# Two attention layers on one core: the first layer's projection as seven products of quarters

## The chip, the core and the metric

The kernel runs on one NeuronCore of a Trainium2 chip. The core has a matrix engine (TensorE, PE in the profile; its weight loads are listed apart as PEld), a vector engine (VectorE, DVE), an activation engine (ScalarE, ACT), a general engine (GpSimd, POOL) and a sequencer that mostly issues transfers (SyncE, SP). Each engine works through its own instruction queue in order; the queues meet only through semaphores. Matmuls write to PSUM, a small memory of banks of 512 four-byte columns on 128 partitions; the other data lie in SBUF, which is 128 partitions wide, or in DRAM. The metric is the time of one execution on the device in microseconds (us).

## The reference

An input of 8 images with 512 channels of 32 x 32 points (1024 tokens) passes through two attention layers. In what follows b is the image ("batch"), C = 512 channels, T = 1024 tokens.

```python
# layer 0: 8 heads of 64 channels
h   = group_norm(x)                            # 32 groups of 16 channels
qkv = einsum('oc,bct->bot', qkv_w, h) + qkv_b
q, k, v = fake_quant(each)                     # 8 bits, range over the whole tensor
w = softmax(q' k * scale);  a = w v            # per head, 1024 x 1024
x = x + einsum('oc,bct->bot', proj_w, a) + proj_b      # the projection

# layer 1: one head of 512 channels
h = group_norm(x)
q, k, v = h wq + bq, h wk + bk, h wv + bv
attn = softmax(q k / sqrt(512));  out = attn v
x = x + out wp + bp
```

The change concerns the line of the projection: a 512 x 512 matrix times 512 channels x 1024 tokens per image, added to the image and a bias per output channel, and the group norm's statistics that are taken from the result.

## The kernel before, in words

A first stage computes q, k and v of all images and keeps them in DRAM. A second stage interleaves the two layers: the generator `attention` runs layer 0's heads for one image ahead, and `others` runs the projection, the second norm and layer 1 for the image before it. Each time `others` yields, one step of `attention` is issued: four score tiles (`scores`, the tiles `st`), their exponentials on ScalarE (`pt`), the split of each into a half-precision cast and a remainder (`two`; the cast on ScalarE, GpSimd or VectorE, the remainder always on VectorE), the products with v (`over_keys`, tiles `av`) and the row sums (`totals`, tiles `sm`). `yield 2` makes the step begin with the products (`late`), `yield -1` makes it begin with two score tiles (`dense`).

The matmul order is the program's own. On VectorE and ScalarE a planner decides: `dve.do` places work at once, and `dve.later` puts a chore with a cost and a due time on a list, from which `fill` takes what fits before the next placed work; `settle` forces all chores of a name. The plan becomes a fixed order of each engine's queue. `awaits` tells the planner when a tile is free; it is no instruction.

Large matrix products outside layer 0 use `seven`: operands in quarters, seven products in place of eight, with sums and differences of quarters made ahead and the results added up in two PSUM tiles x and y that take turns; `keep`, `add` and `whole` empty a tile after each product. Layer 1's products are done so: `g` (a_block), `v2ps` (v_block2), `s` (s_block) and `o` (o_run). In these, `keep` is a copy on ScalarE.

The projection, `project` (line 1296), is not: for each half of the tokens (512 columns) and each of four blocks of 128 output channels it adds four matmuls of 512 columns in one PSUM tile `pj`, and VectorE adds tile, bias and image in one instruction into the image's tile `h` (`evict`, line 1313). A store of the result to DRAM (`x1_d`) and the norm's statistics (`stats`) follow. The weights `wp` come from the input by a 1 MB transfer on ScalarE's queue (`load_wp`, line 1266), for image 0 in pieces on SP's queue (`load_first`). For images 1 to 7 the projection sits inside layer 1 of the image before: in `o_run`, after the fourth of seven products of its second half, `between[0]` (function `first`) runs one attention step, the projection's first half, a step, the second half, and then a `late` step; then comes the fifth product of `o`, and after it the first part of the norm (`norm1`, `norm_steps`). That part is a small matmul `gps` of the channel means with a matrix that averages over groups, then four small VectorE steps, then a second small matmul. PSUM tiles for the projection come from the pool of the score tiles (two tiles of 2 x 512 columns, `score_bank`), for image 0 from the pool `ps_o`.

In the profile all VectorE and ScalarE work carries line 91 and all matmuls line 209, so the names of the tiles tell the steps apart.

## Time and profile before

| quantity | value |
|---|---|
| median of 3 runs | 2557.06 us (2555.32 to 2558.21) |
| profiled execution | 2557.22 us, its span 2555.4 us |
| granted TensorE clock | 0.999 |
| projection matmuls `pj` | 224.0 us busy, in 512 records (256 matmuls) |
| evictions `h<-pj,vec,h` on VectorE | 64, mean 750 ns |
| statistics | 690 ns each, the aggregate 210 ns |
| 1 MB weight transfers `wp` | 7, on ScalarE's queue |
| stores `x_d<-h` | 64 of 256 KB, on SP's queue |
| transfers in all | 250.70 MB, 98 GB/s on average |

The projections can be found in time by their tiles: image 0 from 692.9 us, image 1 from 930.9 and then one every 240 us or so, image 7 from 2363.6. The profile's lines give start and length, engine, instruction, shapes, and in brackets the idle time of the engine before and what ended it. A matmul of four-byte numbers appears as two records, and records of one group overlap, so the spacing of the starts is the better measure of cost. From image 3 on, some matmul records are missing from the trace.

### The profile page before, as it was taken

The numbers are of one execution on the slowest core, as the hardware profiler recorded it, in microseconds if no ns is written. First come the engines' busy times: TensorE is split into PE (matmuls) and PEld (weight loads), VectorE is DVE, ScalarE is ACT, GpSimd is POOL, SyncE is SP. The second block draws the span as 40 slices with busy tenths as digits, with TensorE's granted clock in tenths as the row PEclk, the third lists the DMA queues.
The fourth block names the chain that finished last, engine by engine and source line by source line (L and its number), as shares of the span: only waits on it lengthen the run. The fifth ranks groups of instructions, "written<-read, shape, count | busy, mean of one in ns | idle before, by whom it ended". The sixth has DMA issues, their size and how long they took to land.

```text
span 2555.4 us, 38727 instructions
## 1 busy us (share of the span) xinstructions
PE 2516.6 (98%) x15670; PEld 1746.1 (68%) x15670; DVE 1895.6 (74%) x2746; ACT 1348.2 (53%) x1687; POOL 187.9 (7%) x167
## 2 busy tenths in 40 slices
PE   8999999999999999999999999999999999999998
PEld 4788888873357756775777577657756775777687
DVE  7888776668887778777877787777778777775544
ACT  3332223219856655665667466656665675664122
POOL 0000000001100001000100100010101000100000
PEclk9999999999999999999999999999999999999999
DMA  4533333236622232223223222322232123212211
GB/s 167 178 142 124 132 124 121 110 130 164 164 88 63 79 113 87 59 70 127 92 59 104 84 87 74 109 96 63 80 109 91 55 72 124 87 51 84 87 38 39
DMA packets 160718, 250.70 MB, mean 98 GB/s; under 512 B 27153, under 2 KB 93713, under 8 KB 159121
## 3 DMA queue, kind: packets, MB, share of 16 engines
q1 hardware_dynamic: 125792, 182.81, 21.9%
q10 hardware_dynamic: 30560, 57.71, 6.6%
q0 software_dynamic: 4176, 7.60, 1.7%
q8 instruction: 125, 2.05, 0.3%
q14 instruction: 65, 0.52, 0.1%
HBM read 153.64 MB, written 86.28 MB: 94 GB/s over the span
## 4 chain that ended last, share of the span: by engine, by line
PE 85%; DVE 4%; issue 3%; ACT 2%; DMA 1%; POOL 0%; SPq 0%; ACTq 0%; DVEq 0%; POOLq 0%
PE s L209 15%; PE o L209 13%; PE qkps L209 12%; PE pj L209 8%; PE av L209 8%; PE v2ps L209 7%; PE g L209 6%; PE vps L209 6%; PE st L209 4%; PE sm L209 3%; ACT pt L91 1%; DVE two L91 1%; DVE h L91 1%; PE fold L209 0%; DVE acc L91 0%
## 5 line engine op out<-in xcount | busy, mean ns | idle before, releaser
L91 ACT ACTIVATE pt<-st,esc 128x1024 f32<-128x1024 f32 x467 | 497.1, 1115 | 332.7 <-PE st L209 316.8
L91 DVE TENSOR_TENSOR two<-pt,two 128x1024 f16<-128x1024 f32 x467 | 561.9, 1217 | 131.5 <-POOL two L1092 100.8
L91 ACT CAST two<-pt 128x1024 f16<-128x1024 f32 x346 | 350.8, 1056 | 6.9 <-ACT p L91 5.1
L1092 POOL CAST two<-pt 128x1024 f16<-128x1024 f32 x112 | 147.5, 1317 | 1406.8 <-PE sm L209 745.1
L209 PE MATMUL av<-two,v 128*32 128x512 f16 x3968 | 245.7, 381 | 2.5 <-DVE two L91 2.4
L209 PE MATMUL s<-g,h 128*128 128x256 f32 x1024 | 233.4, 380 | 0.0
L209 PE MATMUL pj<-ao,wp 128*128 128x512 f32 x512 | 224.0, 595 | 0.6 <-DVE h L91 0.6
L209 PEld LDWEIGHTS s<-g,h 128*128 128x128 f32 x1024 | 192.9, 190 | 31.0 <-issue 4.3
L91 ACT ACTIVATE u_ring<-qkps,qkbt 128x512 f32<-128x512 f32 x89 | 61.1, 687 | 243.6 <-PE qkps L209 228.9
L209 PEld LDWEIGHTS <-v 128*32 128x32 f16 x3968 | 92.0, 96 | 139.8 <-issue 66.7
L209 PEld LDWEIGHTS pj<-ao,wp 128*128 128x128 f32 x512 | 96.0, 190 | 122.5 <-issue 112.2
L209 PE MATMUL s<-g,sums 128*128 128x256 f32 x768 | 178.4, 381 | 0.2 <-DVE p L91 0.2
L209 PE MATMUL o<-p,v 128*128 128x256 f32 x768 | 175.2, 382 | 1.0 <-DVE p L91 1.0
L209 PE MATMUL st<-q,k 64*128 64x512 bf16 x1024 | 163.4, 382 | 12.2 <-ACT pt L91 7.8
L209 PEld LDWEIGHTS o<-p,v 128*128 128x128 f32 x768 | 144.3, 190 | 27.1 <-issue 5.7
L209 PEld LDWEIGHTS s<-g,sums 128*128 128x128 f32 x768 | 144.6, 190 | 24.3 <-issue 4.6
L209 PE MATMUL sm<-two,ones 128*32 128x512 f16 x1984 | 136.0, 379 | 0.0
L209 PEld LDWEIGHTS <-k 64*128 64x128 bf16 x1024 | 34.8, 94 | 144.1 <-issue 142.5
L209 PE MATMUL qkps<-half,w_high 128*128 128x512 f32 x480 | 132.5, 398 | 0.0
L209 PE MATMUL qkps<-half,w_mix 128*128 128x512 f32 x480 | 130.6, 394 | 1.0 <-DVE half L91 1.0
L209 PE MATMUL qkps<-half,w_low 128*128 128x512 f32 x480 | 130.5, 394 | 0.0
L209 PE MATMUL v2ps<-wm,h 128*128 128x256 f32 x512 | 119.9, 383 | 1.9 <-ACT g L91 1.3
(228 smaller groups left out, 3903.9 us busy)
## 6 DMA issues: line engine op xcount, KB each, us to landing
rs<-rs_d SPq DMA_DIRECT2D x76, 256.0 KB
x<-in_x_dram SPq DMA_DIRECT2D x32, 512.0 KB
q_d<-wa SPq DMA_DIRECT2D x32, 512.0 KB
k_d<-wa SPq DMA_DIRECT2D x32, 512.0 KB
v_d<-v_ring SPq DMA_DIRECT2D x32, 512.0 KB
raw<-q_d SPq DMA_DIRECT2D x32, 512.0 KB
raw<-k_d SPq DMA_DIRECT2D x32, 512.0 KB
x_d<-h SPq DMA_DIRECT2D x64, 256.0 KB
```

The lines of the kernel that those rows point to most:

```text
L91: ins = self.latest = op(*args, **kw).ins
L209: ins = nc.tensor.matmul(ps, lhsT=lhsT, rhs=rhs, **kw).ins
L1092: copy(two[:, 0], pt)
```

## The change

For images 1 to 7 the projection is computed by `seven`, half by half: the weights' quarters a11, a12, a22 and the sums s1 to s4 on the left, the attention result's quarters and differences on the right. The left operands are made once, during image 0's projection, from its weights (`combine_wp`: four additions on VectorE) and kept in a DRAM tile `wp_d` by four stores; each later image loads six of the seven in one transfer of 1.5 MB and the seventh, s4, apart, into a free part of layer 1's v tile. The right operands are made on VectorE: t1 in place soon after the second pair of heads is divided (`first_sums`), t2 in the v tile at the start of the projection, t3 and t4 in place after the first and second product of each half. Each of the seven products is added by VectorE straight into a quarter of the image's tile, without a copy on ScalarE; the option `alone` of `seven` gives these calls their own turn-taking. Statistics of two channel blocks become due after the sixth product and of the other two after the seventh.

Image 0 keeps the eight products.

The bias is no longer added in the eviction. `norm_steps` takes it as `shift`: it is added to the channel means before the group matmul, and taken off the group mean that is later subtracted from the data. The residual image stored in DRAM then lacks the bias, so it is added to the output bias `ob`.

```diff
--- before.py
+++ after.py
@@ -226,7 +226,8 @@
     def norm_steps(
-        src, dst, wcol, bank, nm, ccs=range(CC), fine=False, put=None, mv=None, apply=None
+        src, dst, wcol, bank, nm, ccs=range(CC), fine=False, put=None, mv=None, apply=None,
+        shift=None,
     ):
@@ -242,6 +243,8 @@
                 if fine and i + 1 < n:
                     yield
         yield
+        if shift is not None:
+            dve.tensor_add(mv[:, :, 0], mv[:, :, 0], shift)
         ps = bank(f"gps_{nm}")[:, 0:n]
         mm(ps, lhsT=gavg, rhs=mv[:, :, 0], start=True, stop=True)
@@ -250,7 +253,10 @@
         def offsets():
             dve.tensor_sub(d, mv[:, :, 0], ps)
-            dve.tensor_copy(mean, ps)
+            if shift is None:
+                dve.tensor_copy(mean, ps)
+            else:
+                dve.tensor_sub(mean, ps, shift)
             dve.tensor_mul(d, d, d)
             dve.tensor_add(d, d, mv[:, :, 1])
@@ -1184,6 +1190,8 @@
                 def divide():
                     dve.scalar_tensor_tensor(aot, aot, scl[:, 2:3], rs, ALU.mult, ALU.mult)
+                    if b and j == 1:
+                        first_sums(b)
                 def spread():
                     r = rcs[:, n * 16 : (n + 1) * 16]
@@ -1264,8 +1272,8 @@
                 dma(xts[b][:, :, bass.ts(hf, 512)], x_v[b, :, :, bass.ts(hf, 512)])
         def load_wp(b, dma):
-            wps[b] = l2p.tile([P, CC, C], F32, tag="sums", name=f"wp0_{b}")
-            dma(wps[b], w_sq[WP0])
+            wps[b] = w = l2p.tile([P, 6, CC // 2, C // 2], F32, tag="sums", name=f"wp0_{b}")
+            dma(w, wp_d[:, 0:6])
         def load_first(u):
@@ -1293,11 +1301,108 @@
             for t, src in zip(wm_tiles(b), wm_d):
                 act.dma_start(t, src)
-        def project(b, bank=bank):
+        wp_d = dram.tile([P, 7, CC // 2, C // 2], F32, tag="wp", name="wp_d")
+        def combine_wp():
+            wc = l2p.tile([P, 3, NT // 2, 256], F32, tag="vsum", name="wp_combined").rearrange(
+                "p a (s k) n -> p (a s) k n", k=2
+            )
+            a11, a12, a21, a22 = (
+                wps[0][:, k * CC // 2 : (k + 1) * CC // 2, m * 256 : (m + 1) * 256]
+                for m in range(2) for k in range(2)
+            )
+            s2, s3, s1, s4 = (wc[:, i] for i in range(4))
+            for args in (
+                (s1, a21, a22, ALU.add), (s2, s1, a11, ALU.subtract),
+                (s3, a11, a21, ALU.subtract), (s4, a12, s2, ALU.subtract),
+            ):
+                dve.later("wc", elements(512), lambda args=args: tt(*args), within=20.0)
+            def keep():
+                nc.sync.dma_start(wp_d[:, 3:7], wc[:, 0:4])
+            dve.later("wc", 0.0, keep, within=20.0)
+            nc.sync.dma_start(wp_d[:, 0], a11)
+            nc.sync.dma_start(wp_d[:, 1], a12)
+            nc.sync.dma_start(wp_d[:, 2], a22)
+        def first_sums(b):
+            for cc in range(CC // 2):
+                h = ao[b, cc]
+                dve.later("at", elements(512), lambda h=h: tt(
+                    h[:, :, 256:512], h[:, :, 256:512], h[:, :, 0:256], ALU.subtract
+                ), within=30.0)
+        def project_seven(b, room):
+            settle("at")
             settle("ao")
+            st, mvs[b] = stat_tiles(CC, f"b{b}")
+            w = wps.pop(b)
+            a11, a12, a22, s2, s3, s1 = (w[:, i] for i in range(6))
+            t2 = room[:, 0 : NT // 2, 0:256].rearrange("p (k h) n -> p k h n", h=NH)
+            s4 = room[:, NT // 2 : NT // 2 + 2, 0:256]
+            nc.sync.dma_start(s4, wp_d[:, 6])
+            left, right = slice(0, 256), slice(256, 512)
+            def second(k):
+                tt(t2[:, k], ao[b, 2 + k][:, :, right], ao[b, k][:, :, right], ALU.subtract)
+            for k in range(2):
+                dve.do(elements(512), lambda k=k: second(k))
+            for hf in range(NH):
+                h11, t1, h21, h22 = (
+                    [ao[b, c + k][:, hf, n] for k in range(2)] for c in (0, 2) for n in (left, right)
+                )
+                th = [t2[:, k, hf] for k in range(2)]
+                q11, q12, q21, q22 = quarters(b, hf)
+                def into(q, row, col, full, hf=hf):
+                    def add(ps):
+                        there = dve.do(elements(512), lambda: tt(q, ps, q, ALU.add))
+                        if full is not None:
+                            nc.sync.dma_start(x1_d[b][row][hf][:, :, col * 256 : (col + 1) * 256], q)
+                        return there
+                    return add
+                def stats(oc, hf=hf):
+                    dve.bn_stats(st[:, oc, hf, :], xts[b][:, oc, bass.ts(hf, 512)])
+                    if hf == NH - 1:
+                        aggregate(mvs[b], st, oc)
+                keeps = [into(q, *at_, None) for q, at_ in ((q11, (0, 0)), (q21, (1, 0)), (q22, (1, 1)))]
+                adds = [into(q, *at_, 1) for q, at_ in ((q11, (0, 0)), (q21, (1, 0)), (q22, (1, 1)))]
+                for step in seven(
+                    f"pj_{b}_{hf}",
+                    ((a11, h11), (a12, h21), (s2, th), (s3, h11), (s1, t1), (s4, h22), (a22, h21)),
+                    lambda n, ps: keeps[n](ps), into(q12, 0, 1, 1), lambda n, ps: adds[n](ps),
+                    score_bank, True,
+                ):
+                    if step in (1, 2):
+                        for k in range(2):
+                            h = (h11, h21)[step - 1][k]
+                            args = (h, th[k], h) if step == 1 else (h, h, th[k])
+                            dve.do(elements(256), lambda args=args: tt(*args, ALU.subtract))
+                    for oc in {6: (2, 3), 7: (0, 1)}.get(step, ()):
+                        dve.later("pj", 0.62 + 0.2 * hf, lambda oc=oc, stats=stats: stats(oc), within=4.0)
+                    chore()
+                if hf + 1 < NH:
+                    yield -1
+            for k in [k for k in ao if k[0] == b]:
+                del ao[k]
+        def project(b, room=None):
+            if b:
+                yield from project_seven(b, room)
+                return
+            settle("ao")
+            combine_wp()
             st, mvs[b] = stat_tiles(CC, f"b{b}")
             wp0 = wps.pop(b)
             for hf in range(NH):
@@ -1311,9 +1416,7 @@
                     xx = xts[b][:, oc, bass.ts(hf, 512)]
                     def evict():
-                        dve.scalar_tensor_tensor(
-                            xx, ps, vec[:, V_PB0 + oc : V_PB0 + oc + 1], xx, ALU.add, ALU.add
-                        )
+                        dve.tensor_tensor(xx, ps, xx, ALU.add)
                         nc.sync.dma_start(x1_d[b][oc // 2][hf][:, oc % 2, :], xx)
                     def stats(oc=oc, hf=hf, xx=xx):
@@ -1359,9 +1462,11 @@
                     put(hf, elements(512), work)
             for n, _ in enumerate(norm_steps(
-                at, at, V_GN1W, bank, f"b{b}", put=put, mv=mvs[b]
+                at, at, V_GN1W, bank, f"b{b}", put=put, mv=mvs[b], shift=vec[:, V_PB0 : V_PB0 + CC]
             )):
                 if n == 2:
+                    if b == 0:
+                        settle("wc")
                     sums[b] = l2p.tile(
                         [P, 3, NH, CC // 2, 256], F32, tag="sums", name=f"sums2_{b}"
                     )
@@ -1390,14 +1495,15 @@
             dve.later("o", 0.25, spread, pe.t + 4.0, 5.0)
             return rs
-        def seven(nm, pairs, keep, whole, add, bank=bank):
+        def seven(nm, pairs, keep, whole, add, bank=bank, alone=False):
             nonlocal turn
-            turn ^= 1
+            turn ^= not alone
+            free, side = ([0.0, 0.0], 0) if alone else (busy, turn)
             x, y = (bank(f"{nm}_{i}").rearrange("p (t n) -> p t n", t=2) for i in range(2))
             def product(n, ps, start):
@@ -1406,7 +1512,8 @@
                 for t in range(2):
                     for i in range(k):
                         mm(
-                            ps[:, t, :], lhsT=left[:, i, bass.ts(t, P)], rhs=right[:, i, :],
+                            ps[:, t, :], lhsT=left[:, i, bass.ts(t, P)],
+                            rhs=right[i] if type(right) is list else right[:, i, :],
                             start=start and t == 0 and i == 0, stop=(i == k - 1),
                             skip_group_check=True,
                         )
@@ -1417,12 +1524,14 @@
                 (5, x, False, whole, None),
             )
             for i, (n, ps, start, out, m) in enumerate(work):
-                awaits(free[(i + turn) % 2])
+                if not alone:
+                    side = turn
+                awaits(free[(i + side) % 2])
                 product(n, ps, start)
-                free[(i + turn) % 2] = out(ps) if m is None else out(m, ps)
+                free[(i + side) % 2] = out(ps) if m is None else out(m, ps)
                 yield i + 1
-        free = [0.0, 0.0]
+        busy = [0.0, 0.0]
         turn = 0
         def slots(gq):
@@ -1773,8 +1882,9 @@
                     def first():
                         nonlocal ahead
                         yield -1
-                        yield from project(b + 1, score_bank)
+                        yield from project(b + 1, vt)
                         yield 2
+                        settle("pj")
                         ahead = norm1(b + 1, score_bank)
                         next(ahead)
@@ -1856,6 +1966,7 @@
                     load_first(24)
                 else:
                     dve.tensor_add(dst, tot, vec[:, V_BP : V_BP + CC])
+                    dve.tensor_add(dst, dst, vec[:, V_PB0 : V_PB0 + CC])
             (m11, m12), (m21, m22), (v1, v2), (v3, v4) = ([t[:, i] for i in range(2)] for t in wm)
             for args in (
                 (v1, m11, m12, ALU.subtract), (v2, m22, v1, ALU.subtract),
```

## The prediction

> **What bounds the kernel now.** First the page's totals, then who TensorE waited for, then the order of time around one projection. The totals:

> ```profile
> PE 2516.6 (98%) x15670; PEld 1746.1 (68%) x15670; DVE 1895.6 (74%) x2746; ACT 1348.2 (53%) x1687; POOL 187.9 (7%) x167
> ```

> TensorE is busy for 98% of the span at a granted clock of 0.999: time is won only by fewer or shorter matmuls, and lost wherever a matmul waits. The list of TensorE's waits is short:

> ```profile
> PE st L209 <- ACT pt L91: 7.8, 15, 0.8
> PE gps_a L209 <- DVE gmv_a L91: 6.9, 1, 6.9
> PE st L209 <- DVE h L91: 3.1, 6, 0.5
> PE av L209 <- DVE two L91: 2.4, 4, 1.6
> ```

> No entry is a transfer. The third is the projection's: six times, 0.52 us each. Here is batch 1 on TensorE, then on VectorE (start, length, instruction, idle before). Two records of a 4-byte matmul are one matmul, so x32 is 16:

> ```profile
> 930.91 14.00 PE L209 MATMUL pj<-ao,wp 128*128 128x512 f32 x32
> 944.84 0.39 PE L209 MATMUL st<-q,k 64*128 64x512 bf16 x2
> 945.75 0.39 PE L209 MATMUL st<-q,k 64*128 64x512 bf16 x2 [0.52 <-DVE h L91]
> ...
> 949.43 14.00 PE L209 MATMUL pj<-ao,wp 128*128 128x512 f32 x32
> 963.36 1.05 PE L209 MATMUL av<-two,v 128*32 128x512 f16 x16
> ...
> 967.27 3.72 PE L209 MATMUL o<-g,vsum 128*128 128x256 f32 x16
> 970.83 0.28 PE L209 MATMUL gps_b<-gmv_b,gavg 128*128 128x4 f32 x2
> 970.97 3.70 PE L209 MATMUL o<-g,v 128*128 128x256 f32 x16
> ```

> ```profile
> 957.39 0.69 DVE L91 BATCH_NORM_STATS2 gst_b<-h 128x6 f32<-128x512 f32 x1
> 958.12 0.21 DVE L91 BATCH_NORM_AGGREGATE gmv_b<-gst_b 128x2 f32<-128x12 f32 x1
> 958.24 1.17 DVE L91 TENSOR_TENSOR two<-pt,two 128x1024 f16<-128x1024 f32 x1
> ...
> 963.47 0.75 DVE L91 SCALAR_TENSOR_TENSOR h<-pj,vec,h 128x512 f32<-128x512 f32 x1 [0.70 <-PE pj L209]
> ...
> 971.03 0.69 DVE L91 TENSOR_TENSOR kept_u<-o,kept_u 128x512 f32<-128x512 f32 x1 [2.78 <-PE o L209]
> 971.64 0.15 DVE L91 TENSOR_TENSOR gd_b<-gmv_b,gps_b 128x4 f32<-128x4 f32 x1
> ```

> To be seen: from the last projection matmul to the matmul of the means (gps) TensorE passes 970.83 - 963.36 = 7.47 us and never waits; VectorE stands idle for 2.78 us ahead of 971.03, so it has room, but its order is fixed. The prices of the two matmul shapes come from undisturbed runs:

> ```profile
> 1041.75 3.62 PE L209 MATMUL s<-g,h 128*128 128x256 f32 x16
> 1045.20 1.89 PE L209 MATMUL s<-g,sums 128*128 128x256 f32 x8
> ...
> 2363.60 27.63 PE L209 MATMUL pj<-ao,wp 128*128 128x512 f32 x64
> 2391.06 3.62 PE L209 MATMUL o<-g,vsum 128*128 128x256 f32 x16
> ```

> A 512-column matmul costs (2391.06 - 2363.60)/32 = 0.858 us, a 256-column one (1045.20 - 1041.75)/8 = 0.431.

> **The change, part by part.**

> *Seven products.* Half a batch was 16 matmuls of 512 columns, 13.73 us; it becomes 28 of 256, 12.08. Gain 1.65 per half, in batches 1 to 7, so 14 times: **-23.1 us**. All of it is on the path.
> [...]

> *Evictions.* VectorE now empties a tile seven times per half, not four, and each product reuses the tile of the one but last. A product lasts 4 x 0.431 = 1.73 us. An eviction begins 0.11 after its product (944.84 to 944.95) and takes 0.69 (TENSOR_TENSOR from the accumulator, 128x512), so it is late only if VectorE reaches it over 0.93 us late. Between evictions stand two subtractions on 256 columns or one 0.75 us quantisation step. No row has a tensor-tensor on 256 columns; it lies between 0.44 (scalar-tensor-tensor on 256) and 0.69 (tensor-tensor on 512), nearest the former by size: two take 0.88, and 0.11 + 0.61 + 0.88 = 1.6 fits in 1.73. Even two at 0.69 would overrun one slot by 0.3, within the 0.93. **Zero**, covered by the next product.
> [...]

> *End of the first half.* The second score tile still waits for the last eviction; that is now 0.69, not 0.75: -0.06 in six batches, **-0.4**. Behind it VectorE has three cast remainders ("two", 1.13 from start to start), three statistics (0.61) and one scaling (0.61) before the next half's first eviction: 0.72 + 3.39 + 1.83 + 0.61 = 6.55 after the product, due at 4.53 + 1.73 + 0.11 = 6.37. Late by 0.2, inside the 0.93.

> *End of the second half, batches 1 to 6.* This is the price. The planner moves four cast remainders and three statistics behind the last eviction, and the new add stands behind one more remainder and behind the eviction of the next attention product; gps waits for the add, and everything on TensorE waits behind gps. From the last projection matmul: eviction 0.11 + 0.61 = 0.72; four remainders 4 x 1.13, to 5.24; three statistics with aggregate at 0.85 (957.39 to 958.24), to 7.79; a remainder, to 8.92; eviction of o, there since about 8, to 9.53; add 0.15 (row gd_b), 9.68; gps 0.06 later, 9.74. Against 7.47 that is 2.27 us, and a wait of about 0.5 of "av" for the second remainder hides inside. **+13.6** in six batches. Bounds: had all statistics drained earlier, only the o eviction and the add remain, 0.11 + 0.61 + 0.15 + 0.06 = 0.93 a batch, 5.6 in all; were the remainders as slow as 1.35 (5.46 for four at 751.88), 1.1 more each, 20 in all. I take the middle, since the row's mean of 467 is 1.217 long, 1.13 spaced.

> *Batch 7* has no attention left beside it: the chain is 3.27, the o product ends at 3.46 (2391.06 to 2394.52), then 0.93: **+0.9**.

> *Batch 0* keeps eight products. One combination of the weights (0.61) is put ahead of the first eviction, for which TensorE waited already (0.65 us at 700.81): +0.6; the other three fit in 2.38 us of idle before 715.95. The add delays gps, which waited at 728.03 for the last aggregate, by about 0.1. **+0.7**, between -0.1 and +2.5 if all four counted.

> *Hidden by what.* The difference t1 of the quarters (two, 0.61 each) takes the place of a 1.13 us subtraction that moves behind; VectorE is idle 1.5 us before 1059.94 there. The t2 sums (two) are done about 1.3 us into the projection; the third product needs them at 3.45. The mean's copy becomes a subtraction of the same size, and the output bias gets one 0.15 us add at 742, where VectorE idled 1.57.

> *Transfers and queues.* Weights: one 1.5 MB transfer for 1 MB, issued at 907.95, used at 930.91; between 910 and 919 the transfers ran at about 400 GB/s and then nearly nothing did, so 1.3 us more for it and for x behind it ends 9 us early. On SP's queue the 256 KB load of s4 waits for the attention's second product (over at 918.6); what stands behind it, the row sums, is ready only at 923, and s4 is used as the last product, 10 us in. The eight stores per batch have half-length pieces and stand ahead of the v load, which is used half a projection later; the next reader of h waits 15 us. In batch 0 four stores (1.75 MB) join SP's queue among loads with tens of us to spare. POOL's queue is unchanged. Zero each; were the cover gone, a microsecond per batch.

> **Sum.** -23.1 - 0.4 + 13.6 + 0.9 + 0.7 = -8.3. The profiled execution took 2557.22, the median is 2557.06: **2548.9 us**.

> **The rivals.**
> - *The means wait for one eviction alone.* If the drain is short or overlapped, the loss is 5.6, not 13.6: 2540.9. For it: VectorE idles 30% of this stretch. Against: its order is fixed, and nine instructions stand ahead of the add.
> - *A wash.* The drain runs at the slow rows and batch 0 loses its 2.5: -23.1 - 0.4 + 20 + 0.9 + 2.5 = 0: about 2557. For it: rows of 1.5 us for steps of 0.75, beside POOL's casts. Against: the remainder's mean of 1.217.
> - *Slower: the two tiles bind.* Each product waits for the eviction of the one but last, five waits a half, 70 in all. It decides from 0.93 us of lateness; slower by 5 us needs 13.4/70 = 0.19 beyond that, so VectorE 1.1 late at each: then 2562. For it: a quantisation step at 1.5 instead of 0.75 comes near. Against: that is one step in a few.
> - *It does not act.* The eight products stay or the weights come late: no gain. Against: the weights' 23 us, worked out above; I give it no chance of its own.

> **How the numbers follow.** Forecast 0.45 (2544 to 2552), one-eviction rival 0.20, wash 0.23, slower 0.12. About 0.2%, 5.1 us, is what a measurement of this kernel can tell from no change; so faster 0.65, same 0.23, slower 0.12. The range takes in the one-eviction and the wash cases, 2541 to 2559, leaving some 0.1 on each side.

> **What would show it.** Projection matmuls at 0.431 us, 12.1 us per half; the second score tile waiting 0.46; gps in batches 1 to 6 waiting for VectorE by 1.5 to 2 us, in batch 7 by 0.9; no wait between products. The prediction is wrong if matmuls of pj wait for h, if gps starts at once, or if quarter matmuls cost more than 0.44.

## The result and the profile after: slower by 0.4%

The changed kernel takes 2566.08 us (median of 7 runs, 2563.96 to 2567.96), the kernel before on the same chip 2557.41 us (7 runs, 2555.32 to 2559.03). The ratio is 1.0037, with a 95% interval of 1.0027 to 1.0046: slower by about 9 us, where 8 us less were forecast. The profiled execution took 2566.47 us with a span of 2564.7, which is 9.3 longer than the span before.

The page's totals, the granted clock of the core (span, then clock), and the longest of TensorE's waits (total us, times, longest):

```profile
PE 2507.1 (98%) x16006; PEld 1816.7 (71%) x16006; DVE 1968.4 (77%) x2885; ACT 1349.7 (53%) x1687; POOL 188.2 (7%) x167
...
core 0: 2564.7 us, clock 0.995
...
PE gps_b L209 <- DVE gmv_b L91: 14.2, 8, 2.2
...
PE av L209 <- DVE two L91: 4.2, 9, 1.5
```

TensorE still fills 98% of the span, but the first entry of the list is new: the matmul of the means waits for VectorE in every image, 14.2 us in all. And the clock is 0.995, not 0.999. Here is image 1 on TensorE, second half of the projection and what follows (start, length, idle before in brackets):

```profile
949.13 3.72 PE L209 MATMUL pj<-ao,wp 128*128 128x256 f32 x16
952.69 1.89 PE L209 MATMUL pj<-v,wp 128*128 128x256 f32 x8
954.41 5.34 PE L209 MATMUL pj<-ao,wp 128*128 128x256 f32 x24
959.59 1.89 PE L209 MATMUL pj<-ao,v 128*128 128x256 f32 x8
961.41 1.05 PE L209 MATMUL av<-two,v 128*32 128x512 f16 x16
...
966.06 3.72 PE L209 MATMUL o<-g,vsum 128*128 128x256 f32 x16
971.94 0.35 PE L209 MATMUL gps_b<-gmv_b,gavg 128*128 128x4 f32 x2 [2.16 <-DVE gmv_b L91]
972.16 5.39 PE L209 MATMUL o<-g,v 128*128 128x256 f32 x16
977.38 0.28 PE L209 MATMUL gps_b<-gd_b,gavg 128*128 128x4 f32 x2
```

The half takes 961.41 - 949.13 = 12.28 us, against 13.93 before: the matmuls became shorter as forecast. Then TensorE idles for 2.16 us ahead of the means. And the next product of o, eight matmuls of 256 columns, takes 5.39 us where before it took 3.70 with the same matmuls and no wait inside. What VectorE did meanwhile:

```profile
961.52 0.69 DVE L91 TENSOR_TENSOR h<-pj,h 128x512 f32<-128x512 f32 x1
962.13 5.46 DVE L91 TENSOR_TENSOR two<-pt,two 128x1024 f16<-128x1024 f32 x4
967.51 0.68 DVE L91 BATCH_NORM_STATS2 gst_b<-h 128x6 f32<-128x512 f32 x1
...
969.83 0.21 DVE L91 BATCH_NORM_AGGREGATE gmv_b<-gst_b 128x2 f32<-128x12 f32 x1
969.95 1.17 DVE L91 TENSOR_TENSOR two<-pt,two 128x1024 f16<-128x1024 f32 x1
971.04 0.68 DVE L91 TENSOR_TENSOR kept_u<-o,kept_u 128x512 f32<-128x512 f32 x1
971.64 0.15 DVE L91 TENSOR_TENSOR gmv_b<-gmv_b,vec 128x4 f32<-128x4 f32 x1
```

This is the drain of the prediction, in its order: the last eviction, four remainders, three statistics, a remainder, the eviction of o, and only then the add of 0.15 us, on which the means and with them all of TensorE wait.

The long product is a matter of the clock. The trace records when the granted clock changes; it falls to a half at 973.1, 1215.5, 1696.7, 1939.1 and 2181.4 us (and once at 689.8, and once more after the last matmul), each time but the last for exactly 3.41 us, and all these times lie a multiple of 3.413 us apart ((1215.5 - 973.1)/3.413 = 71.0). So I cut the time into that grid. Columns: the stretch, its length, busy time of TensorE with its instructions, granted clock, then the share of the transfer engines and GB/s:

```profile
686.39:689.80 3.41, 1.53 (x16) 1.00 0.39 50
689.80:693.22 3.42, 2.88 (x24) 0.50 1.06 258
...
969.70:973.11 3.41, 1.25 (x8) 1.00 0.30 84
973.11:976.52 3.41, 3.41 (x10) 0.50 0.27 84
1212.04:1215.46 3.42, 1.45 (x8) 1.00 0.27 81
1215.46:1218.87 3.41, 3.41 (x10) 0.50 0.28 91
...
1450.98:1454.39 3.41, 2.94 (x14) 1.00 0.00 1
1454.39:1457.80 3.41, 1.73 (x9) 1.00 0.28 81
1457.80:1461.22 3.42, 3.42 (x19) 1.00 0.36 119
```

In images 1 and 2 TensorE was busy for 1.25 and 1.45 us of an interval (ahead of image 0's projection, for 1.53), and the next interval ran at half clock. In images 1 and 2 that was fully busy: 3.41/2 = 1.7 us lost. In image 3 the same wait of 2.16 us fell across two intervals, the emptier one had 1.73 us of work, and the clock stayed. This is why image 3 alone, of images 1 to 6, has no long product.

Where the 9.3 us come from, by the starts of the same matmuls in the two traces:

| part | forecast | profile |
|---|---|---|
| projection matmuls, images 1 to 7 | -23.1 | -22.5 |
| between the halves, images 1 to 6 | -0.4 | +2.0 (0.33 each) |
| last projection matmul to the means, images 1 to 6 | +13.6 | +18.4 (10.53 - 7.47 = 3.06 each) |
| product after the means: half clock in five of six images | not in the sum | +8.9 (5 x 1.76 + 0.1) |
| image 7, last projection matmul to the means | +0.9 | +1.2 |
| image 0, up to the first projection matmul of image 1 | +0.7 | +1.0 |
| from the last eviction to the end of the program | not in the sum | +1.9 |
| rest: the stretches between one norm and the next projection | 0 | -1.5 |
| sum | -8.3 | +9.4 |

### The profile page after: what moved, and what is told of

It is laid out like the page before. It is cut to its first block, busy times and chain, and to the rows that moved or that the text cites. A ratio compares the mean times of both kernels' runs of the same rounds, so it can differ in the third digit from the quotient of the medians.

```text
span 2564.7 us, 39621 instructions
## 1 busy us (share of the span) xinstructions
PE 2507.1 (98%) x16006; PEld 1816.7 (71%) x16006; DVE 1968.4 (77%) x2885; ACT 1349.7 (53%) x1687; POOL 188.2 (7%) x167
## 4 chain that ended last, share of the span: by engine, by line
PE 80%; DVE 10%; issue 2%; ACT 2%; DMA 1%; POOL 1%; SPq 0%; DVEq 0%; ACTq 0%; POOLq 0%
PE s L209 15%; PE o L209 13%; PE qkps L209 12%; PE pj L209 7%; PE v2ps L209 7%; PE av L209 7%; PE vps L209 6%; PE g L209 5%; DVE two L91 4%; PE st L209 4%; PE sm L209 3%; DVE h L91 1%; ACT pt L91 1%; DVE sums L91 1%; DVE kept_u L91 1%
## 5 line engine op out<-in xcount | busy, mean ns | idle before, releaser
L91 ACT ACTIVATE pt<-st,esc 128x1024 f32<-128x1024 f32 x467 | 498.7, 1114 | 337.5 <-PE st L209 248.7
L91 DVE TENSOR_TENSOR two<-pt,two 128x1024 f16<-128x1024 f32 x467 | 569.5, 1239 | 114.8 <-POOL two L1098 81.8
L91 ACT CAST two<-pt 128x1024 f16<-128x1024 f32 x346 | 350.6, 1054 | 10.2 <-issue 4.0
L209 PE MATMUL av<-two,v 128*32 128x512 f16 x3968 | 247.6, 382 | 4.5 <-DVE two L91 4.2
L209 PE MATMUL s<-g,h 128*128 128x256 f32 x1024 | 233.4, 380 | 0.0
L209 PEld LDWEIGHTS s<-g,h 128*128 128x128 f32 x1024 | 192.9, 190 | 31.0 <-issue 4.3
L209 PEld LDWEIGHTS <-v 128*32 128x32 f16 x3968 | 92.5, 96 | 140.4 <-issue 67.5
L91 ACT ACTIVATE u_ring<-qkps,qkbt 128x512 f32<-128x512 f32 x89 | 61.0, 685 | 243.7 <-PE qkps L209 221.3
L209 PE MATMUL s<-g,sums 128*128 128x256 f32 x768 | 178.4, 381 | 0.2 <-DVE p L91 0.2
L209 PE MATMUL st<-q,k 64*128 64x512 bf16 x1024 | 165.7, 382 | 13.0 <-ACT pt L91 8.7
L209 PE MATMUL o<-p,v 128*128 128x256 f32 x768 | 175.2, 382 | 1.0 <-DVE p L91 1.0
L209 PEld LDWEIGHTS o<-p,v 128*128 128x128 f32 x768 | 144.3, 190 | 27.1 <-issue 5.7
L209 PEld LDWEIGHTS s<-g,sums 128*128 128x128 f32 x768 | 144.7, 190 | 24.2 <-issue 4.6
L209 PE MATMUL pj<-ao,wp 128*128 128x256 f32 (+1 forms) x624 | 155.0, 403 | 0.2 <-DVE h L91 0.2
L209 PEld LDWEIGHTS pj<-ao,wp 128*128 128x128 f32 x624 | 117.3, 190 | 34.7 <-issue 19.8
L209 PEld LDWEIGHTS <-k 64*128 64x128 bf16 x1024 | 35.4, 94 | 145.5 <-issue 144.6
L209 PE MATMUL sm<-two,ones 128*32 128x512 f16 x1984 | 136.5, 380 | 0.0
L209 PE MATMUL qkps<-half,w_high 128*128 128x512 f32 x480 | 132.5, 398 | 0.0
L209 PE MATMUL qkps<-half,w_mix 128*128 128x512 f32 x480 | 130.6, 394 | 1.0 <-DVE half L91 1.0
L209 PE MATMUL qkps<-half,w_low 128*128 128x512 f32 x480 | 130.5, 394 | 0.0
L209 PE MATMUL v2ps<-wm,h 128*128 128x256 f32 x512 | 119.9, 383 | 1.9 <-ACT g L91 1.3
```

Source lines behind the costliest of these rows:

```text
L91: ins = self.latest = op(*args, **kw).ins
L209: ins = nc.tensor.matmul(ps, lhsT=lhsT, rhs=rhs, **kw).ins
```

## The experiments

**Theory A:** the means wait for what is queued ahead of the add, and a wait that leaves TensorE mostly idle in one interval of 3.41 us halves the clock in the next. **Theory B:** the half clock comes from something else, such as the quarter matmuls. **Theory C:** the loss sits elsewhere in the seven products. The ratios below are to the kernel before, run on the same chip: 2557.11 us (21 runs) for the first four, 2556.84 us (13 runs) for the other three.

**1. The add alone moved forward** (`add_early`).

```diff
+        if shift is not None:
+            dve.tensor_add(mv[:, :, 0], mv[:, :, 0], shift)
         yield
-        if shift is not None:
-            dve.tensor_add(mv[:, :, 0], mv[:, :, 0], shift)
         ps = bank(f"gps_{nm}")[:, 0:n]
```

> The add of the bias to the means is placed right behind the last aggregate, ahead of a cast remainder and of the eviction of o's fifth product; nothing else changes. Theory A (the means wait for what is queued on VectorE ahead of the add, and a wait of 2.16 us lying in one 3.41 us interval is followed by an interval at half clock): the matmul of the means comes 8.86 instead of 10.53 us after the last projection matmul, its wait falls from 2.16 to about 0.5 us, so 6 x 1.67 = 10.0 us, and no interval at half clock follows (5 x 1.7 = 8.5 us): about 2547.5 us, 7 to 10 us faster than before. Theory B (the half clock has another cause, such as the denser quarter matmuls): the wait goes, the half clock stays, about 2556 us. Theory C (the loss sits elsewhere in the seven products): about 2566 us.

Measured: 2547.89 us (6 runs), ratio 0.9966 (0.9953 to 0.9978). On TensorE in image 1 of this kernel:

```profile
968.96 0.36 PE L209 MATMUL gps_b<-gmv_b,gavg 128*128 128x4 f32 x2 [0.59 <-DVE gmv_b L91]
969.18 3.70 PE L209 MATMUL o<-g,v 128*128 128x256 f32 x16
```

The wait is 0.59 us, the product after it 3.70, the clock 0.999 over the span, and the means come 8.96 us after the last projection matmul. One instruction of 0.15 us, moved past a remainder and an eviction, is worth 18 us. With it the seven products are faster than the kernel before. Theory C falls.

**2. The wait filled with work of no use** (`filled_wait`): the kernel computes the reference's result and, beside it, eight matmuls that nobody reads.

```diff
-        ps = bank(f"gps_{nm}")[:, 0:n]
+        room = bank(f"gps_{nm}")
+        if shift is not None and nm != "b0":
+            at = pe.t
+            for _ in range(8):
+                mm(room[:, 128:256], lhsT=gavg, rhs=ones, start=True, stop=True)
+            pe.t = at
+        ps = room[:, 0:n]
```

> The changed kernel with eight matmuls of 128 columns, results unused, put on TensorE ahead of the matmul of the means in images 1 to 7: they take about 1.7 us of the 2.16 us for which TensorE would wait, and wait for nothing on VectorE. Theory A: the means' matmul starts when it did (10.5 us after the last projection matmul), but no half clock follows: 5 x 1.7 = 8.5 us less, about 2557.5 us; image 7 loses up to 0.8 us. Theory B (half clock has another cause) or if only the wait itself costs: 2566 us.

Measured: 2558.34 us (10 runs), ratio 1.0006 (0.9996 to 1.0016), 7.7 us less than the changed kernel for more work. Image 1 of this kernel on TensorE:

```profile
967.18 1.95 PE L209 MATMUL gps_b<-ones,gavg 128*128 128x128 f32 x16
969.41 0.39 PE L209 MATMUL gps_b<-gmv_b,gavg 128*128 128x4 f32 x2 [0.29 <-DVE gmv_b L91]
969.66 3.70 PE L209 MATMUL o<-g,v 128*128 128x256 f32 x16
```

The means come 10.44 us after the last projection matmul, as late as in the changed kernel (10.53), so VectorE's chain is what it was. But the idle time is gone, the clock stays whole (0.999), and the next product takes 3.70 us. Wait and half clock are thereby priced apart: about 10 us for the wait that `add_early` removed, about 8 for the clock. Theory B falls.

**3. Eight products and only the bias moved** (`eight_and_shift`): the kernel before with plain additions as evictions, and with the change's add, subtraction and output bias.

```diff
-                        dve.scalar_tensor_tensor(
-                            xx, ps, vec[:, V_PB0 + oc : V_PB0 + oc + 1], xx, ALU.add, ALU.add
-                        )
+                        dve.tensor_tensor(xx, ps, xx, ALU.add)
...
+        if shift is not None:
+            dve.tensor_add(mv[:, :, 0], mv[:, :, 0], shift)
         ps = bank(f"gps_{nm}")[:, 0:n]
```

> Eight products as before, with the bias moved alone: plain additions as evictions, the add of the bias to the means where the change has it. Theory A: the add stands behind the eviction of o's fifth product, which ends at 971.64 in the trace of before, so the means' matmul comes at 971.9 instead of 970.83: 6 x 1.1 = 6.4 us of waits of 1.1 us, no half clock, about 2563.5 us: slower than before by 6 us without any of the seven products. If the moved bias costs nothing: 2557 us.

Measured: 2564.50 us (8 runs), ratio 1.0029 (1.0018 to 1.0040). On VectorE in image 1 of this kernel:

```profile
965.24 0.21 DVE L91 BATCH_NORM_AGGREGATE gmv_b<-gst_b 128x2 f32<-128x12 f32 x1
967.34 1.23 DVE L91 TENSOR_TENSOR two<-pt,two 128x1024 f16<-128x1024 f32 x1 [1.90 <-POOL two L1098]
971.35 0.69 DVE L91 TENSOR_TENSOR kept_u<-o,kept_u 128x512 f32<-128x512 f32 x1 [2.77 <-PE o L209]
971.95 0.15 DVE L91 TENSOR_TENSOR gmv_b<-gmv_b,vec 128x4 f32<-128x4 f32 x1
```

The last aggregate is done at 965.45 and the add could have run in any of the 1.90 and 2.77 us for which VectorE then idles. It runs at 971.95, because it stands behind the eviction of o, which needs the product that TensorE makes just ahead of the means. The means come 8.57 us after the last projection matmul, not 7.47; no half clock follows. So the moved bias, as placed, costs 7 us by itself, on an engine with 4.67 us of idle time ahead of it.

**4. The drain put in another order** (`order_mended`): the late statistics and the add ahead of the two remainders that belong to the following attention step.

```diff
-        if shift is not None:
+        if shift is not None and nm == "b0":
             dve.tensor_add(mv[:, :, 0], mv[:, :, 0], shift)
...
                     over_keys((u + 2, u + 3))
+                    dve.settle("pj")
                     totals((u + 2, u + 3))
...
+            dve.later("pj", 0.15, lambda mv=mvs[b]: dve.tensor_add(
+                mv[:, :, 0], mv[:, :, 0], vec[:, V_PB0 : V_PB0 + CC]
+            ), within=4.0)
```

> The changed kernel with the three late statistics and the add placed behind the two remainders that the next av needs, ahead of the two remainders of the following step. Theory A: the add ends about 6.0 us after the last projection matmul, TensorE reaches the means at 8.4, so it does not wait and the clock stays: 2557.2 - 22.5 for the matmuls + 2 for waits at the end of the first half + 2 for the av wait + 1 for image 0 = about 2540 us, faster than both. Rival: the two remainders that now come later hold the buffers of the exponentials, and the next score tiles wait for them by 1 us or more in each image: about 2548 us.

Measured: 2565.60 us (6 runs), ratio 1.0035 (1.0022 to 1.0048). The forecast was out by 25 us, although the part it spoke of worked: the means come 8.20 us after the last projection matmul and wait for nothing. Another wait took their place. The waits of TensorE in this kernel, a line of TensorE and three of VectorE and ScalarE in image 1:

```profile
PE g L209 <- ACT vsum L91: 13.3, 6, 2.2
...
985.14 1.99 PE L209 MATMUL g<-sums,wa 128*128 128x256 f32 x8 [2.21 <-ACT vsum L91]
...
972.59 0.18 DVE L91 TENSOR_TENSOR rcs<-apart 128x16 f32<-128x16 f32 x1 [3.65 <-DMA apart<-rs]
...
982.11 2.25 ACT L91 ACTIVATE pt<-st,esc 128x1024 f32<-128x1024 f32 x2 [4.37 <-DVE two L91]
984.25 0.83 ACT L91 ACTIVATE vsum<-g,gb 128x256 f32<-128x256 f32 x2
```

VectorE's new plan put the next remainders behind a step that waits 3.65 us for a transfer. The remainders hold the buffers of the exponentials, so ScalarE starts the next two only after 4.37 us of waiting, and `vsum`, which frees a PSUM tile of g, is queued behind them. TensorE waits 2.2 us in each of six images, and after four of these waits (images 2, 3, 4 and 6) the clock was halved. It is the same fault one step later: a short instruction queued behind a long wait.

**5. The same order, with those remainders put into VectorE's idle time** (`order_mended_2`).

```diff
         dve.do(0.6, offsets)
+        if shift is not None and nm != "b0":
+            dve.settle("sum")
         yield
```

> As the kernel with the order mended, and the two remainders that its plan put behind the row sums' transfer now stand right behind the means' steps, where VectorE idled for 3.65 us. Theory: the wait of g for ScalarE's vsum, 2.2 us in each of six images with four half clocks after it, came from these late remainders (exponential late, vsum queued behind it); without it 2565.6 - 13.3 - 6.8 = about 2545 us. If g waits for vsum all the same, 2560 us or more.

Measured: 2541.06 us (4 runs, 2540.30 to 2544.55), ratio 0.9936 (0.9920 to 0.9953), the fastest of all. In image 1 of this kernel TensorE runs through:

```profile
971.12 0.29 PE L209 MATMUL gps_b<-gmv_b,gavg 128*128 128x4 f32 x2
971.27 3.70 PE L209 MATMUL o<-g,v 128*128 128x256 f32 x16
```

Neither the wait for `gmv_b` nor that for `vsum` is left in images 1 to 6. Of the 22.5 us that the matmuls save, 16 arrive. The profiled execution is the longest of the four, 2544.55 us: ahead of image 0's projection its clock was at a half for two intervals, 6.83 us from 689.63.

**6. One cast taken from GpSimd** (`cast_on_act`). Of the four remainders in the drain one takes 2.06 us, from 965.53 to 967.59, and the others about 1.2. GpSimd casts from 964.61 to 966.51, in 1.90 us, where the same cast took 1.04 in the kernel before (at 965.95, with VectorE idle).

```diff
-                elif s % 4 == 2:
+                elif s % 4 == 2 and (b < 2 or (j, hf, s) != (1, 0, 2)):
                     cast(nc.gpsimd.tensor_copy)
```

> The changed kernel with one cast in images 2 to 7 of the attention (the third step of the second pair's first half, the one that runs on GpSimd beside the four remainders ahead of the statistics) on ScalarE instead. If the remainder of 2.06 us is long because GpSimd's cast runs beside it, all four take about 1.15 us and the drain is 0.9 us shorter; the planner also puts the next remainder behind the means, 1.1 us more. The means then come 9.3 us after the last projection matmul instead of 10.53, wait 0.95 us, and no half clock follows: about 2566 - 7.4 - 8.5 = 2550 us. If the remainder is long for another reason, the four still take 5.4 us. The price of ScalarE's added cast, 1.0 us an image, may come back as a wait of a later product: up to 2556 us.

Measured: 2561.08 us (10 runs), ratio 1.0015 (1.0006 to 1.0025). VectorE's drain in image 1 of this kernel, remainders that come later, and two new waits of TensorE:

```profile
961.52 4.62 DVE L91 TENSOR_TENSOR two<-pt,two 128x1024 f16<-128x1024 f32 x4
...
979.49 3.49 DVE L91 TENSOR_TENSOR two<-pt,two 128x1024 f16<-128x1024 f32 x3
...
980.76 0.40 PE L209 MATMUL av<-two,v 128*32 128x512 f16 x4 [0.89 <-DVE two L91]
988.35 2.00 PE L209 MATMUL g<-h,wa 128*128 128x256 f32 x8 [0.41 <-DVE g L91]
```

The four remainders take 4.62 us instead of 5.46, so GpSimd's cast was the cause; the means come 9.32 us after the last projection matmul and wait 0.94; no half clock follows any of these waits. All three numbers were forecast. The time was not: 2550 had been expected. TensorE now waits for VectorE 0.89 + 0.41 = 1.3 us more in each image. Of the remainders that follow the drain, the changed kernel runs one ahead of the means (at 969.95); here it stands behind them, which the expectation counted as a gain of 1.1 us, and from 979.49 three remainders run in a row where the changed kernel has two (from 983.00). ScalarE's casts were over at 972.09, long before. So the waits are those of a longer row in VectorE's queue; that moving the remainder caused them is read from the order and was not tried. Some 0.6 us more in each image has no place that I know.

**7. Waits of growing length** (`clock_ladder`): behind the early add, the means are multiplied by one several times, so that each image waits longer.

```diff
             dve.tensor_add(mv[:, :, 0], mv[:, :, 0], shift)
+            for _ in range((0, 2, 4, 5, 6, 8, 11, 0)[int(nm[1:])]):
+                dve.tensor_scalar(mv[:, :, 0], mv[:, :, 0], 1.0, None, ALU.mult)
```

> The kernel with the early add (its means wait 0.59 us in images 1 to 6), and behind the add 2, 4, 5, 6, 8 and 11 multiplications of the means by one in images 1 to 6, each about 0.15 to 0.2 us: waits of some 1.0, 1.3, 1.5, 1.7, 2.1 and 2.7 us on TensorE. Theory A (the clock is halved for the 3.41 us interval after one in which TensorE idled for most of it): no half clock in images 1 and 2, a half clock in image 6, and the change comes between 1.7 and 2.2 us, depending on where the wait lies in the interval. Theory B (the half clock does not depend on the wait's length): drops anywhere or nowhere.

Measured: one run, 2557.37 us. The waits were 1.01, 1.42, 1.62, 1.82, 2.24 and 2.84 us in images 1 to 6; the clock was halved after the last two only. Its grid for images 3 to 6, columns as above:

```profile
1445.62:1449.03 3.41, 1.79 (x10) 1.00 0.28 80
1449.03:1452.44 3.41, 3.41 (x18) 1.00 0.05 4
1684.55:1687.96 3.41, 1.98 (x10) 1.00 0.23 74
...
1926.90:1930.31 3.41, 1.17 (x7) 1.00 0.29 82
1930.31:1933.72 3.41, 3.41 (x10) 0.50 0.03 2
2169.24:2172.66 3.42, 0.65 (x4) 1.00 0.31 84
2172.66:2176.07 3.41, 3.41 (x10) 0.50 0.03 2
```

With 1.79 us of work in an interval the clock stayed, with 1.17 it fell; in the changed kernel it fell with 1.53 and stayed with 1.73. From these four figures alone one would estimate a limit near half of 3.41 us, but busy time does not give a sharp one. In `order_mended` the wait of 2.2 us left 1.64 and 1.49 us of work in an interval of images 1 and 5, and the clock stayed; in `order_mended_2` it fell after 1.72, ahead of image 0's projection. The interval of image 5 in `order_mended` and the one after it, then the two of `order_mended_2`:

```profile
1950.68:1954.09 3.41, 1.49 (x7) 1.00 0.00 0
1954.09:1957.50 3.41, 3.12 (x14) 1.00 0.15 8
...
686.21:689.63 3.42, 1.72 (x20) 1.00 0.32 42
689.63:693.04 3.41, 2.70 (x24) 0.50 1.09 266
```

Over all nine traces, from 20 us after the start on, an interval with 1.45 us of work or less was always followed by one at half clock and one with 1.73 or more never. Between these two figures both happened. What else decides there is open.

## Why the prediction was wrong

*Seven products.* Right: 28 matmuls of 256 columns took 12.28 us a half where 12.08 was forecast, and the gain was 22.5 of 23.1 us.

*Evictions.* Right. Of all evictions only one made a projection matmul wait, 0.24 us in image 7. A subtraction on 256 columns, for which the prediction had no row, took 0.41 us, less than the 0.44 it was priced at; two at 0.69 would have overrun their slot by 0.11 + 0.61 + 1.38 - 1.73 = 0.37 us, not 0.3, still within the 0.93. The rival in which the two tiles bind did not happen, though the total came out near its number.

*End of the first half.* The wait for the last eviction fell by 0.06 us as forecast (0.46 for 0.52). Missed was a second wait for an exponential, 0.21 us of idle time and 0.39 us by the starts, since the remainders that free its buffer are drained there too: +2.0 us instead of -0.4.

*End of the second half, images 1 to 6.* The mechanism was right, in its order and to 0.8 us: 10.53 us to the means where 9.74 was worked out. The term that was mis-sized is "four remainders 4 x 1.13": they took 5.38 us, at the upper bound that the text named, because one of them, of 2.06 us, runs beside GpSimd's cast. That makes +18.4 instead of +13.6.

*The step that failed* is the one that turned this wait into time. I priced 2.27 us of waiting at 2.27 us, and read the granted clock of 0.999 as a constant. From 20 us on it fell in the changed kernel after every interval with 1.53 us of work or less, and no interval of the kernel before had so little (the emptiest, from 20 us on and up to the last matmul, has 2.00 us of work, the one from 685.27 to 688.68). After the wait the next interval ran at half clock, 1.7 us more in five of six images, 8.9 us in all, and `filled_wait` shows that this is the clock and not the chain.

*Sum.* With the terms as measured, the sum without the 8.9 us of the clock would have been about +0.5 us (-0.8 without the 1.3 us of image 0, told below, as well): the "wash" among my rivals. The clock's 8.9 us took it beyond the range's upper end of 2559. The rival on the far side named the wrong mechanism.

*Image 7* came as forecast (+1.2 for +0.9). *Image 0* came close by accident: the combination ahead of the first eviction cost nothing (the 0.65 us wait is gone), and some 1.3 us came from the half clock at 689.8 us, just ahead of the projection. Before had a wait of 1.58 us at the same place and no half clock. Its grid can be read as well, from the fall of the clock after the last matmul, at 2552.36: 546 intervals of 3.4133 us ahead of it lies a boundary at 688.7, which cuts the wait (688.17 to 689.75) in two, and the emptier interval keeps 2.00 us of work. So whether image 0 pays depends on where the grid lies in an execution; the changed kernel's profile shows one that paid.

*Transfers.* No matmul waited for one. But from the last eviction to the end of the program the changed kernel takes 7.6 us and the one before 5.7; all seven kernels with seven products take 7.2 to 7.8 there, the one with eight 5.8. Why is open; no run was aimed at it.

## What to carry to other kernels

A tiny instruction that another engine waits for has to stand where its operands are ready, not where the code that uses it begins: in these queues it inherited every wait ahead of it (in `eight_and_shift` 971.95 - 965.45 = 6.50 us), even on an engine that is idle a quarter of the time. Where an engine's clock falls after a stretch of little work, as TensorE's did here, price a new wait twice, once for itself (here 2.16 us) and once for what runs slower after it (here 1.7); if the wait can't be removed, work of no use in its place can still pay (7.7 us in `filled_wait`). And a queue put in a new order needs the question again for the next short instruction in it: `order_mended` moved the fault, `order_mended_2` removed it.

## What the runs showed of the hardware

In the drain of image 1 a remainder on VectorE and a cast on GpSimd took longer while both ran. A remainder began at 964.40 and took 1.22 us, the next one began at 965.53 and took 2.06; the cast that had begun at 964.61 took 1.90 and ended at 966.51, and the second remainder ended 1.08 us after it. In the kernel before, the cast at 965.95 took 1.04 with VectorE idle, and the remainder at 967.03, begun as that cast ended, took 1.23. So the meeting cost about 0.86 us of the cast (1.90 - 1.04) and about 0.83 of the second remainder (2.06 - 1.23). With the cast on ScalarE (`cast_on_act`) the four remainders took 4.62 us instead of 5.46, 0.84 less. How the two hold each other up was not shown.
